# Layer 3 of a four-layer graph network: scores in rows, exponentials by head, squares exchanged through DRAM, no adding transfers

## The chip, the cores and the metric

The kernel runs on one core of a Trainium2 chip. Its time is the device time of one execution in microseconds (us); the number to compare is the median of several executions. The engines of the core are called PE (TensorE, matrix products and transpositions through them), DVE (VectorE), ACT (ScalarE), POOL (GpSimd) and SP (SyncE, which here only issues transfers). All data are 32-bit floats.

## The reference

There are 128 graphs of 128 nodes with 512 features. Four attention layers follow each other, each with a layer norm and a ReLU before it and the input added after it. Layers 0 and 2 have one head; layer 1 has two attentions, of 4 heads of 256 and of one head of 512; layer 3 has 8 heads of 64. Layer 3, which the change is about, is in short:

```python
h  = relu(layernorm(x))                                  # 128 nodes x 512
xh = (h @ W_proj).reshape(128, 8, 64)                    # values by head
a_src, a_dst = <xh, W_att[:, :64]>, <xh, W_att[:, 64:]>  # 128 x 8 each
s   = leaky_relu(a_src[i] + a_dst[j] + b, 0.2)           # by head, 128 x 128
att = softmax(where(A[i, j] > 0, s, -1e30), over j)
x   = x + relu(att @ xh)                                 # heads side by side
```

## The kernel before

Each graph is one stream of steps (`graph(b)`, line 983 and on): load, layer 0, layer 1, layer 2, layer 3, store. A graph's 128 nodes lie on the 128 partitions. Up to `FLYING = 11` graphs are in work at once. The order on every engine is made when the program is built: a scheduler (`Scheduler`, `issue`) holds a list of streams, gives each step a planned time from costs in `Step.estimate` and the buffers it needs from pools, and each time writes out the next step of the stream whose planned start is earliest, or, among those nearly as early, the one most overdue. A due time is the graph's age times the busiest engine's planned load, plus its place in the graph (`plan`, `rank`). On the chip each engine runs its instructions strictly in the written order, waiting where data are not there. A `Fork` starts a side stream, a `Join` waits for it; `Group` keeps steps together. All steps are issued at line 301, so the profile's groups are told apart by tile names.

Layers 0 and 2 call `attended`: the scores' row part is a PE transposition of a broadcast column, DVE adds the mask and takes the maximum in one instruction, ACT makes the exponentials, PE transposes them (`transposed`, with a copy by ACT) and multiplies. Layer 1 has its row part written to DRAM and read back broadcast to all partitions (`rows_in_dram`, four small writes and one load on SP), then the same by head; the 4 x 128 x 128 weights are transposed in two moves: DVE transposes all 32 x 32 squares in place, and `turned` exchanges the squares through DRAM (four writes and one load on SP).

Layer 3 before keeps the scores of each head with the source node j on the partitions, so that they go into PE without a transposition. `graph` takes the transposed mask from the PE transposition that layer 1 needs anyway, as `m3t` (11 buffers). `layer3` copies it eight times into `e` (tile of 128 x 8 x 128, 3 buffers) with one ACT instruction. PE projects (16 products of two passes), ACT copies to `fx` (tile x3), POOL adds the bias into `f`. `rows_in_dram` writes both score parts as rows; SP loads the j part into `d`, broadcast, and POOL adds the i part onto `e` with an accumulating transfer (`added`). DVE runs eight mask-and-maximum instructions on `d` for the largest score of each row and head, `mx`; POOL, ACT and POOL turn it into minus the largest score. Those go to DRAM as rows as well, and a second accumulating transfer adds them to `e` after ACT's eight Prelu instructions, which bring in the j part as a bias. One Exp over all 1024 columns follows, then PE multiplies with the values; a column of ones beside each head's values gives the sum of the weights, by which DVE divides.

The last `LATE = 5` graphs have no transfers in their chains: rows come from PE (`spread`, transpositions of broadcast columns into a bank of PSUM), and `add_rows` has DVE add them to `e`, once for the i part and once for minus the largest score.

Of the kernel before, what the change touches and what calls it, by code (L numbers as in the profile page):

```python
# [9 lines left out]
F32 = mybir.dt.float32  # L10
I32 = mybir.dt.int32
AF = mybir.ActivationFunctionType
ALU = mybir.AluOpType
# [31 lines left out]
class Step:  # L45
# [19 lines left out]
    def estimate(self, name, outs, ins, kw):  # L65

        if name == "dma_start":
            moved = size(outs[0]) * outs[0].shape[0] * 4
            if self.engine == "POOL":
                self.moves = moved / 165e3  # L70
                return 1.0, 3
            run = 4 * min(a.shape[-1] for a in outs + ins)
            self.moves = moved / (280e3 if run > 512 else 220e3)
            busy = 0.5 if max(len(a.shape) for a in outs + ins) > 2 else 0.35
            return busy, (2.2 if moved > 16384 else 0.6)
# [250 lines left out]
def kernel(  # L326
# [54 lines left out]
    def tile_of(tag, bufs, *shape):  # L381
        return Take(work, [P, *shape], tag, bufs)
# [44 lines left out]
    def setup():  # L427
# [7 lines left out]
        for c in range(KC):  # L435
            if c % 2 == 0:
                pair = yield tile_of("e3", 3, H3, P)
                pair = pair.rearrange("p h q -> p (h q)").rearrange("p (c f) -> p c f", c=2)
            w0.append(pair[:, c % 2])
            yield S.dma_start(out=w0[c], in_=l0_w[c * P : (c + 1) * P])  # L440
# [25 lines left out]
        wa = yield tile_of("e3", 3, H3, P)  # L466
        wa = wa.rearrange("p h q -> p (h q)")[:, : H3 * 2 * K3]
# [120 lines left out]
    def turned(t, squares, tag, bufs):  # L588

        yield V.transpose(squares, squares)
        f = t.shape[1] // R
        d = dram.tile([R, Q, R, f], F32, tag="turned", name="turned")
        yield Group(
            [
                S.dma_start(
                    out=d[:, :, r].rearrange("m b f -> b m f"),
                    in_=t[r * Q : (r + 1) * Q].rearrange("b (m f) -> b m f", m=R),
                )  # L600
                for r in range(R)
            ]
        )
        to = yield tile_of(tag, bufs, R * f)
        yield S.dma_start(out=to, in_=d.rearrange("m b r f -> (m b) (r f)"))
        return to
# [33 lines left out]

    def add_rows(cols, to):

        for g in range(0, cols.shape[1], 4):
            pt = yield from spread(cols[:, g : g + 4])
            part = to[:, g * P : (g + 4) * P]
            yield V.tensor_tensor(part, pt, part, ALU.add)
            give_back(pt)

    def added(to, rows):

        yield G.dma_start(out=to, in_=rows, accum_op=ALU.add)
# [120 lines left out]
    def layer1(xt, mask, late):  # L772
# [28 lines left out]
        else:  # L801
            to = yield from turned(e, e, "et1", 2)
# [57 lines left out]
    def layer3(xt, mask, mask_t, late):  # L860

# [8 lines left out]

        e = yield tile_of("e3", 3, H3, P)
        yield A.copy(e, mask_t.unsqueeze(1).to_broadcast([P, H3, P]))
        give_back(mask_t)
# [11 lines left out]
        yield G.tensor_tensor(f, fx[:, :, :E3].rearrange("p h s -> p s h"), b_l3, ALU.add)  # L885
        if late:
            fork = yield Fork(add_rows(f[:, 1], e.rearrange("p h q -> p (h q)")))
        else:
            rows = yield from rows_in_dram(repeated(f.rearrange("p s h -> p (s h)")), 2 * H3)
            d = yield tile_of("d3", 2, H3, P)  # L890
            yield S.dma_start(out=d.rearrange("p h q -> p (h q)"), in_=rows[:, : H3 * P])
            fork = yield Fork(added(e.rearrange("p h q -> p (h q)"), rows[:, H3 * P :]))

        for g in range(0, H3, 4):
            if late:
                d = yield from spread(f[:, 0, g : g + 4])
                part = d.rearrange("p (h q) -> p h q", h=4)
            else:
                part = d[:, g : g + 4]
# [3 lines left out]
                        out=part[:, j],  # L903
                        in0=part[:, j],
                        in1=mask,
# [9 lines left out]
            if late:  # L915
                give_back(d)
        give_back(mask)
        if not late:
            give_back(d)
        yield Join(fork)  # L920
# [3 lines left out]
        fork = None if late else (yield Fork(rows_in_dram(repeated(mx), H3)))  # L924
        for k in range(H3):
            yield A.activation(
                out=e[:, k, :],
                in_=e[:, k, :],
                func=AF.Prelu,
                bias=f[:, 0, k : k + 1],  # L930
                alpha=SLOPE,
            )
        ef = e.rearrange("p h q -> p (h q)")
        fork = yield Fork(add_rows(mx, ef) if late else added(ef, (yield Join(fork))))
        yield Join(fork)
        yield A.activation(out=ef, in_=ef, func=AF.Exp)
        t = yield tile_of("t", 5, D)
        for i in range(2):
# [6 lines left out]
                        lhsT=e[:, k, :],  # L945
# [16 lines left out]
        give_back(e, fx, f)  # L962
        yield V.scalar_tensor_tensor(xt, t, 0.0, xt, ALU.max, ALU.add)
# [19 lines left out]
    def graph(b):  # L983
# [9 lines left out]
        m3t = yield tile_of("m3t", FLYING, P)  # L993
# [5 lines left out]
        yield A.copy(m3t, pt[:, :P])  # L999
# [9 lines left out]
        yield from layer3(xt, m3, m3t, b >= B - LATE)  # L1009
# [65 lines left out]
```

## Time and profile before

| | |
|---|---|
| Time, median of 3 executions | 3332.38 us (3332.28 to 3333.03) |
| Profiled execution | 3333.2 us, span 3331.4 us |
| Instructions | 59808 |
| PE, DVE, ACT, POOL busy, share of the span | 99%, 83%, 74%, 36% |
| Share of 16 DMA engines: SP's queue, POOL's queue | 25.7%, 20.8% |
| Moved | 380.90 MB, mean 114 GB/s |

How to read it: the profile is one execution recorded by the hardware. PE's matmuls are pipelined and their records overlap, so that a busy PE may still be one that waits a little; the distances between starts tell more. A group is all instructions of one form on the same tiles, and its line gives engine, operation, output and inputs, shapes, count, busy time of all together, the mean of one in ns, and the idle time of the engine just before them with what ended it. PEclk is the clock that PE was granted, in tenths of full speed.

### The profile page before, as it was taken

How to read it: one execution, taken by the hardware profiler on the slowest of the kernel's cores; microseconds unless marked ns; L12 is line 12 of the kernel's file. 1: busy time of each engine (PE TensorE's matmuls, PEld its weight loads, DVE VectorE, ACT ScalarE, POOL GpSimd, SP SyncE). 2: the span in 40 equal slices, each digit the busy share in tenths (PEclk: the TensorE clock that was granted, in tenths of full speed). 3: DMA queues.
4: the chain of work that ended last, by engine and by line, in shares of the span. 5: the costliest groups of instructions: out<-in, count | busy, mean ns of one | idle time of the engine just before them, and what ended most of it. 6: DMA issues, size and time to landing. Idle time of an engine off the chain costs nothing. (4 is left out here: it accounts for less than half of the span.)

```text
span 3331.4 us, 59808 instructions
## 1 busy us (share of the span) xinstructions
PE 3286.5 (99%) x16252; PEld 2577.7 (77%) x16252; DVE 2752.8 (83%) x11063; ACT 2478.1 (74%) x6932; POOL 1208.4 (36%) x2559
## 2 busy tenths in 40 slices
PE   7999999999999999999999999999999999999997
PEld 5777777777777777777777777777777777777776
DVE  5878888888888888888888888888888888888866
ACT  4677777777777777777777777777777777777764
POOL 1233343343343343333334334334334334334321
PEclk7999999999999999999999999999999999999998
DMA  5144444454445454454545454445445545545430
GB/s 156 50 111 116 118 122 115 121 121 119 113 123 121 116 124 119 114 125 114 120 121 120 116 118 121 121 115 123 118 115 124 121 115 120 121 114 123 93 85 29
DMA packets 253730, 380.90 MB, mean 114 GB/s; under 512 B 59088, under 2 KB 138448, under 8 KB 253392
## 3 DMA queue, kind: packets, MB, share of 16 engines
q1 hardware_dynamic: 213792, 248.06, 25.7%
q0 software_dynamic: 35424, 128.99, 20.8%
q8 instruction: 130, 2.13, 0.3%
q14 instruction: 208, 1.70, 0.2%
q10 hardware_dynamic: 4176, 0.02, 0.1%
HBM read 309.35 MB, written 67.57 MB: 113 GB/s over the span
## 5 line engine op out<-in xcount | busy, mean ns | idle before, releaser
L301 PE MATMUL bank<-w2x,y 128*128 128x257 f32 x4096 | 972.1, 380 | 0.0
L301 PE MATMUL bank<-w1x,ht 128*128 128x344 f32 x3072 | 957.4, 455 | 0.7 <-ACT ht L301 0.7
L301 PEld LDWEIGHTS bank<-w2x,y 128*128 128x128 f32 x4096 | 759.4, 190 | 218.5 <-issue 119.6
L301 PEld LDWEIGHTS bank<-w1x,ht 128*128 128x128 f32 x3072 | 567.7, 191 | 243.3 <-issue 7.8
L301 ACT ACTIVATE h<-xt,st 128x512 f32<-128x512 f32 x512 | 416.5, 814 | 257.4 <-POOL st L301 256.2
L301 POOL TENSOR_SCALAR st<-st 128x1 f32<-128x1 f32 x1024 | 351.4, 347 | 661.8 <-DVE st L301 539.5
L301 ACT ACTIVATE e<-e,c 128x128 f32<-128x128 f32 x1408 | 532.7, 400 | 77.8 <-DVE e L301 59.0
L301 PE MATMUL bank<-wpx,ht 128*128 128x264 f32 x2048 | 501.9, 389 | 1.7 <-ACT ht L301 1.7
L301 PEld LDWEIGHTS bank<-wpx,ht 128*128 128x128 f32 x2048 | 390.5, 191 | 66.5 <-ACT ht L301 2.4
L301 ACT ACTIVATE e<-e,f 128x128 f32<-128x128 f32 x1152 | 386.1, 392 | 2.6 <-POOL st L301 1.5
L301 POOL DMA_DIRECT2D e<-d x246 | 233.3, 948 | 389.1 <-DMA d<-r 208.7
L301 DVE BATCH_NORM_STATS2 st<-xt 128x6 f32<-128x512 f32 x512 | 349.4, 683 | 0.0
L301 PEld LDWEIGHTS bank<-x,e 128*128 128x128 f32 x2048 | 269.4, 193 | 91.4 <-issue 56.7
L301 POOL TENSOR_TENSOR st<-st,minus_half 128x1 f32<-128x1 f32 x512 | 298.5, 585 | 29.4
L301 PE MATMUL bank<-et,xl 128*128 128x128 f32 x2048 | 270.3, 275 | 0.0
L301 PE MATMUL bank<-x,e 128*128 128x65 f32 x2048 | 259.0, 270 | 8.9 <-ACT e L301 8.9
L301 POOL TENSOR_TENSOR f<-f 128x8 f32<-128x8 f32 x128 | 30.7, 240 | 651.3 <-DVE f L301 449.1
L301 PE MATMUL bank<-h,et 128*128 128x512 f32 x512 | 263.8, 597 | 1.8 <-ACT et L301 1.8
L301 PEld LDWEIGHTS bank<-et,xl 128*128 128x128 f32 x2048 | 254.0, 192 | 4.9 <-issue 0.5
L301 DVE TENSOR_TENSOR y<-bank,b 128x512 f32<-128x512 f32 x256 | 176.1, 688 | 97.3 <-PE bank L301 95.8
L301 DVE CUSTOM_DVE_ANT_0 d<-d,m 128x128 f32<-128x128 f32 x984 | 225.3, 284 | 34.9 <-DMA d<-d 33.8
L301 POOL TENSOR_SCALAR m<-m 128x128 f32<-128x128 f32 x128 | 143.3, 1119 | 288.9 <-DVE m L301 266.1
(86 smaller groups left out, 5334.4 us busy)
## 6 DMA issues: line engine op xcount, KB each, us to landing
e<-d POOLq DMA_DIRECT2D x246, 512.0 KB, 7.1
d<-d SPq DMA_DIRECT2D x123, 512.0 KB
xt<-in_x_dram SPq DMA_DIRECT2D x128, 256.0 KB
e<-d SPq DMA_DIRECT2D x128, 256.0 KB
out_dram<-xt SPq DMA_DIRECT2D x128, 256.0 KB
turned<-e SPq DMA_DIRECT2D x492, 64.0 KB
et<-turned SPq DMA_DIRECT2D x123, 256.0 KB
at<-in_adj_dram SPq DMA_DIRECT2D x32, 256.0 KB
```

What stands on the lines that cost most here:

```text
L301: method(*args, **kw)
```

## The change

Layer 3's scores are kept with the target node i on the partitions, in rows, as layer 1's are. `m3t`, its copy, the eightfold copy into `e`, `add_rows` and `added` go away. Only the j part goes through DRAM as rows, and SP loads it straight into `e`, in an order where the 32-column pieces of all heads lie together (`heads_inside`). DVE's mask-and-maximum instructions write their sums back into `e`. ACT then runs eight Prelu with the i part as bias, and eight Exp with minus the largest score as bias, in place of one Exp. For the transposition, `turned` becomes `exchanged`, without the DVE step: layer 1 still transposes its squares before the exchange; layer 3 exchanges 128 x 1024 values first (four writes of 128 KB with runs of 1 KB, one load of 512 KB into the new tile `et3` with 2 buffers, which takes the place of `d3`), and then DVE transposes all squares from `et3` back into `e` with one instruction that also puts the pieces in order of heads. In the late graphs `spread` makes the j rows, DVE writes sums from PSUM into `e`, and PE transposes the eight heads with two copies by ACT into `ht` tiles. `layer3` takes `e` after the projection instead of before it. In the scheduler the planned delay of a small transfer goes from 0.6 to 1.3 us, which the order of everything else is made with too.

```diff
@@ -72,7 +72,7 @@
             run = 4 * min(a.shape[-1] for a in outs + ins)
             self.moves = moved / (280e3 if run > 512 else 220e3)
             busy = 0.5 if max(len(a.shape) for a in outs + ins) > 2 else 0.35
-            return busy, (2.2 if moved > 16384 else 0.6)
+            return busy, (2.2 if moved > 16384 else 1.3)
         n = max(size(a) for a in outs[:1] + ins)
         if self.engine == "PE":
             if name == "transpose":
@@ -434,8 +434,8 @@
         w0 = []
         for c in range(KC):
             if c % 2 == 0:
-                pair = yield tile_of("e3", 3, H3, P)
-                pair = pair.rearrange("p h q -> p (h q)").rearrange("p (c f) -> p c f", c=2)
+                pair = yield tile_of("e3", 3, H3 * P)
+                pair = pair.rearrange("p (c f) -> p c f", c=2)
             w0.append(pair[:, c % 2])
             yield S.dma_start(out=w0[c], in_=l0_w[c * P : (c + 1) * P])
         yield Fork(fold_u(w0))
@@ -463,8 +463,8 @@
                 out=wpx[c][:, :, E3:],
                 in_=l3_wp[c * P : (c + 1) * P].rearrange("p (h k) -> p h k", h=H3),
             )
-        wa = yield tile_of("e3", 3, H3, P)
-        wa = wa.rearrange("p h q -> p (h q)")[:, : H3 * 2 * K3]
+        wa = yield tile_of("e3", 3, H3 * P)
+        wa = wa[:, : H3 * 2 * K3]
         yield S.dma_start(out=wa, in_=l3_watt.rearrange("h k -> (h k)").partition_broadcast(P))
         yield Fork(fold_w3(wa), 6)
         for b in range(6, min(FLYING + AHEAD, B)):
@@ -585,13 +585,11 @@
         give_back(pt)
         return blocks_of(r)
 
-    def turned(t, squares, tag, bufs):
-
-
-
-        yield V.transpose(squares, squares)
+    def exchanged(t, tag, bufs):
+
+
         f = t.shape[1] // R
-        d = dram.tile([R, Q, R, f], F32, tag="turned", name="turned")
+        d = dram.tile([R, Q, R, f], F32, tag=f"exchanged{f}", name="exchanged")
         yield Group(
             [
                 S.dma_start(
@@ -637,18 +635,6 @@
             ]
         )
         return pt
-
-    def add_rows(cols, to):
-
-        for g in range(0, cols.shape[1], 4):
-            pt = yield from spread(cols[:, g : g + 4])
-            part = to[:, g * P : (g + 4) * P]
-            yield V.tensor_tensor(part, pt, part, ALU.add)
-            give_back(pt)
-
-    def added(to, rows):
-
-        yield G.dma_start(out=to, in_=rows, accum_op=ALU.add)
 
     def attention(own, rows, e, mask, exact=False):
 
@@ -799,7 +785,9 @@
         if late:
             et = yield from transposed(blocks_of(e), "et1", 2)
         else:
-            to = yield from turned(e, e, "et1", 2)
+
+            yield V.transpose(e, e)
+            to = yield from exchanged(e, "et1", 2)
             et = to.rearrange("p (r h b) -> p h r b", h=H1, b=Q)
             et = [et[:, j] for j in range(H1)]
         give_back(e)
@@ -857,8 +845,7 @@
         yield V.scalar_tensor_tensor(xt, pa, rz, xt, ALU.mult, ALU.add)
         give_back(pa, c)
 
-    def layer3(xt, mask, mask_t, late):
-
+    def layer3(xt, mask, late):
 
         h = yield from norm_relu(xt)
         ht = yield from transposed(blocks_of(h), "ht", 3)
@@ -867,10 +854,6 @@
 
         fx = yield tile_of("x3", 3, H3, E3 + K3 + 1)
         yield G.memset(fx[:, :, E3 + K3 :], 1.0)
-
-        e = yield tile_of("e3", 3, H3, P)
-        yield A.copy(e, mask_t.unsqueeze(1).to_broadcast([P, H3, P]))
-        give_back(mask_t)
         half = H3 // 2
         yield from projected(
             ht,
@@ -883,26 +866,28 @@
         f = yield tile_of("f3", 4, 4, H3)
         f, mx, rz = f[:, :2], f[:, 2], f[:, 3]
         yield G.tensor_tensor(f, fx[:, :, :E3].rearrange("p h s -> p s h"), b_l3, ALU.add)
+
+        e = yield tile_of("e3", 3, H3 * P)
         if late:
-            fork = yield Fork(add_rows(f[:, 1], e.rearrange("p h q -> p (h q)")))
+            heads = e.rearrange("p (h c b) -> p h c b", h=H3, b=Q)
         else:
-            rows = yield from rows_in_dram(repeated(f.rearrange("p s h -> p (s h)")), 2 * H3)
-            d = yield tile_of("d3", 2, H3, P)
-            yield S.dma_start(out=d.rearrange("p h q -> p (h q)"), in_=rows[:, : H3 * P])
-            fork = yield Fork(added(e.rearrange("p h q -> p (h q)"), rows[:, H3 * P :]))
+            heads = e.rearrange("p (c h b) -> p h c b", h=H3, b=Q)
+            rows = yield from rows_in_dram(repeated(f[:, 0]), H3, True)
+            yield S.dma_start(out=e, in_=rows)
+        mask3 = mask.rearrange("p (c b) -> p c b", b=Q)
 
         for g in range(0, H3, 4):
+            part = [heads[:, g + j] for j in range(4)]
             if late:
-                d = yield from spread(f[:, 0, g : g + 4])
-                part = d.rearrange("p (h q) -> p h q", h=4)
-            else:
-                part = d[:, g : g + 4]
+                pt = yield from spread(f[:, 0, g : g + 4])
+                part = pt.rearrange("p (h c b) -> p h c b", h=4, b=Q)
+                part = [part[:, j] for j in range(4)]
             yield Group(
                 [
                     V.tensor_tensor_reduce(
-                        out=part[:, j],
-                        in0=part[:, j],
-                        in1=mask,
+                        out=heads[:, g + j],
+                        in0=part[j],
+                        in1=mask3,
                         scale=1.0,
                         scalar=LOWEST,
                         op0=ALU.add,
@@ -913,27 +898,29 @@
                 ]
             )
             if late:
-                give_back(d)
+                give_back(pt)
         give_back(mask)
-        if not late:
-            give_back(d)
-        yield Join(fork)
         yield G.tensor_tensor(mx, mx, f[:, 1], ALU.add)
         yield A.activation(out=mx, in_=mx, func=AF.Prelu, alpha=SLOPE)
         yield G.tensor_scalar(mx, mx, -1.0, None, ALU.mult)
-        fork = None if late else (yield Fork(rows_in_dram(repeated(mx), H3)))
-        for k in range(H3):
-            yield A.activation(
-                out=e[:, k, :],
-                in_=e[:, k, :],
-                func=AF.Prelu,
-                bias=f[:, 0, k : k + 1],
-                alpha=SLOPE,
+        for bias, func in ((f[:, 1], dict(func=AF.Prelu, alpha=SLOPE)), (mx, dict(func=AF.Exp))):
+            for k in range(H3):
+                yield A.activation(
+                    out=heads[:, k], in_=heads[:, k], bias=bias[:, k : k + 1], **func
+                )
+        et = []
+        if late:
+            for g in range(0, H3, 4):
+                et += yield from transposed(blocks_of(e)[g : g + 4], "ht", 3)
+        else:
+            to = yield from exchanged(e, "et3", 2)
+
+            yield V.transpose(
+                e.rearrange("p (h r b) -> p r h b", h=H3, b=Q),
+                to.rearrange("p (r h b) -> p r h b", h=H3, b=Q),
             )
-        ef = e.rearrange("p h q -> p (h q)")
-        fork = yield Fork(add_rows(mx, ef) if late else added(ef, (yield Join(fork))))
-        yield Join(fork)
-        yield A.activation(out=ef, in_=ef, func=AF.Exp)
+            give_back(to)
+            et = blocks_of(e)
         t = yield tile_of("t", 5, D)
         for i in range(2):
             pa = yield bank()
@@ -942,7 +929,7 @@
                 [
                     T.matmul(
                         p3[:, k - i * half, :],
-                        lhsT=e[:, k, :],
+                        lhsT=et[k],
                         rhs=fx[:, k, E3:],
                         start=True,
                         stop=True,
@@ -960,6 +947,8 @@
             )
             give_back(pa)
         give_back(e, fx, f)
+        if late:
+            give_back(et[0], et[4])
         yield V.scalar_tensor_tensor(xt, t, 0.0, xt, ALU.max, ALU.add)
         give_back(t)
 
@@ -990,13 +979,11 @@
         yield from layer0(xt, m0)
         give_back(m0)
         m3 = yield from not_above_0(a)
-        m3t = yield tile_of("m3t", FLYING, P)
         m1 = yield tile_of("m1", 8, P)
         pt = yield bank()
         yield T.transpose(pt[:, :P], m3, ident)
         give_back(m3)
         yield V.tensor_tensor(m1, pt[:, :P], off_diag, ALU.mult)
-        yield A.copy(m3t, pt[:, :P])
         give_back(pt)
         yield from layer1(xt, m1, b >= B - LATE)
         give_back(m1)
@@ -1006,7 +993,7 @@
         yield from layer2(xt, m2)
         give_back(m2)
         m3 = yield from not_above_0(a)
-        yield from layer3(xt, m3, m3t, b >= B - LATE)
+        yield from layer3(xt, m3, b >= B - LATE)
         yield S.dma_start(out=out[b], in_=xt)
 
     adjs, xs = {}, {}
```

## The prediction

> **What bounds the kernel now.** I read the page's busy shares first, then its slices, then the same busy times in three stretches (columns: stretch, length, then busy time and count per engine, TensorE's granted clock, DMA share, GB/s), then who TensorE waited for inside those stretches.
>
> ```profile
> PE 3286.5 (99%) x16252; PEld 2577.7 (77%) x16252; DVE 2752.8 (83%) x11063; ACT 2478.1 (74%) x6932; POOL 1208.4 (36%) x2559
> ...
> PEclk7999999999999999999999999999999999999998
> ```
> ```profile
> 0.00:100.00 100.00, 77.93 (x274) 51.32 (x275) 62.88 (x211) 47.80 (x126) 14.41 (x42) 0.81 0.47 140
> 100.00:3200.00 3100.00, 3099.47 (x15388) 2436.53 (x15387) 2602.42 (x10533) 2362.70 (x6632) 1165.68 (x2442) 1.00 0.48 116
> 3200.00:3332.00 132.00, 109.08 (x593) 89.88 (x591) 87.47 (x322) 67.60 (x176) 28.32 (x75) 0.91 0.19 48
> ```
>
> PE's waits in the middle 3100 us, then in the last 132:
>
> ```profile
> PE bank L301 <- ACT et L301: 0.4, 1, 0.4
> ```
> ```profile
> PE bank L301 <- ACT e L301: 8.9, 4, 2.7
> PE bank L301 <- ACT h L301: 3.6, 4, 2.1
> PE bank L301 <- POOL f L301: 2.8, 3, 1.7
> ```
>
> A busy PE could still hide waits, since matmuls overlap, so I took start-to-start distances from PE's timeline around 1600 us: 290 ns for 344 columns, 222 for 264, 216 for 257, 430 for 512, 111 for 128 in a run, 104 for 65, 110 for one transposition. Per graph that is 24 x 0.290 + 32 x 0.216 + 16 x 0.222 + 6 x 0.43 + 16 x 0.111 + 16 x 0.104 + 15 x 0.110 = 25.1 us, and graphs do leave every 25.1 us of PE work. So the middle is PE work and nothing else: no other engine's saving can shorten it, while a new wait would lengthen it. Summing starts against these distances, PE loses 41 us in the first 100 us (weights arriving, and a half clock), 13 in the middle 3100 (0.2 in 50), 31 in the last 132. Only head, tail and PE's own instruction count can get shorter.
>
> **What the change costs on each engine.** The rows (busy total, mean ns, idle before):
>
> ```profile
> L301 ACT ACTIVATE e<-e,f 128x128 f32<-128x128 f32 x1152 | 386.1, 392 | 2.6 <-POOL st L301 1.5 <-DMA e<-d 0.8 <-DVE c L301 0.2
> L301 POOL DMA_DIRECT2D e<-d x246 | 233.3, 948 | 389.1 <-DMA d<-r 208.7 <-ACT e L301 155.6 <-issue 18.7
> L301 ACT ACTIVATE e<-e 128x1024 f32<-128x1024 f32 x128 | 134.5, 1051 | 15.3 <-DVE e L301 12.0 <-DMA e<-d 3.3
> L301 ACT COPY e<-m3t 128x1024 f32<-128x1024 f32 x128 | 132.2, 1033 | 0.0
> L301 DVE STREAM_TRANSPOSE e<-e 128x512 f32<-128x512 f32 x123 | 85.3, 693 | 2.0 <-ACT e L301 1.8
> L301 ACT COPY m3t<-bank 128x128 f32<-128x128 f32 x128 | 33.9, 265 | 38.9 <-DVE m L301 38.0
> L301 DVE STREAM_TRANSPOSE r<-f 128x32 f32<-128x32 f32 x246 | 50.8, 207 | 34.8 <-POOL f L301 26.4
> L301 DVE TENSOR_TENSOR e<-bank,e 128x512 f32<-128x512 f32 x20 | 13.3, 685 | 6.2 <-PE bank L301 5.3 <-ACT e L301 0.7
> ```
>
> *ACT*, per graph: out go two mask copies (1.03 + 0.27) and one Exp over 1024 (1.05), 2.35 us; in come eight Exps over 128 with a bias, like the e<-e,f row, 386.1/1152 = 0.335 us each, 2.68. Net +0.33: from 2362.7/3100 x 25.1 = 19.1 us of 25.1 to 19.5. [...]
>
> *DVE*: one of two 32-column transpositions goes (0.21), a 1024-column one comes. No row has it; the 32- and 512-column rows give 0.207 + 992 x (0.693 - 0.207)/480 = 1.21 us. Its operands are cut in 32-element pieces; the mask-and-max reductions are 284 ns whole (d,m) and 286 in such pieces (layer 1's e,m), so I take 1.21, with twice that, 2.4, as the upper end and the 512-column 0.69 as the lower. DVE goes from 21.1 us of 25.1 to 22.1 (23.3).
>
> *POOL* loses two adding transfers a graph, 1.9 us, and the waits in front of them, 389 us in all, which stood before the norm steps queued behind. Nobody in the middle waits for that on PE, so I credit nothing.
>
> *SP* issues 10 transfers for layer 3 instead of 9 (row writes 4, row load 1, square writes 4, square load 1); at 0.3 to 0.43 us each it stays near 8 us of 25. New on its queue is a wait for the last Exp, before the four square writes. Queued behind in the built order are the square load, the next layer-1 rows and layer 1's own square writes; who waits is PE, for layer 1's matmuls. These come 60.6 us of PE work after the projection that feeds them, 47.8 before. DMA bytes stay near 381 MB, without the 20.8% share of the adding queue.
>
> *Layer 3's chain.* From its projection to its attention matmuls the built orders put 36.5 us of PE work before and 62.8 after. The need: x copy, bias, r, row writes and load as the chain of waits has them near 3213 us (0.37 + 0.43 + 0.21 + 1.34 + 1.44 + 4.80) 8.6; eight reductions 2.3; POOL, ACT, POOL 1.0; sixteen activations 5.4; four square writes 1.7 to issue and 1.4 (as a row write) to 4.8 (as a load) to land; load 4.8; transposition 1.2 to 2.4. That is 26 to 32 us, against 62.8: over 30 us of cover for queueing. Before it was some 24 (the adding transfers land in 7.1) against 36.5, and PE never waited. So I cost the middle at 0 in the likely case. If the cover goes, 0.1 us a graph costs 12 us over some 117 graphs.
>
> *PE*: each of the five late graphs loses 24 spread transpositions and gains 8 + 8, 40 fewer at 0.107 = -4.3 us. The built orders put 1.3 of that after the last graph's layer-1 projection, where PE waits anyway; the other 3.0 lie where PE is nearly full. **-3.0.**
>
> **The tail.** The last graph alone sets the end; the late chain runs on chip. Timeline lines of before:
>
> ```profile
> 3297.72 2.66 DVE L301 TENSOR_TENSOR e<-bank,e 128x512 f32<-128x512 f32 x4
> ...
> 3300.43 0.69 DVE L301 BATCH_NORM_STATS2 st<-xt 128x6 f32<-128x512 f32 x1
> ...
> 3323.06 3.68 PE L301 MATMUL bank<-x,e 128*128 128x65 f32 x16 [2.74 <-ACT e L301]
> ...
> 3327.45 0.69 DVE L301 SCALAR_TENSOR_TENSOR xt<-t,xt 128x512 f32<-128x512 f32 x1
> ```
>
> Four adds stand between the last graph's layer-2 result and its statistics; they go, and a 0.2 us mask step stays: -2.4. Then the projection no longer meets PE at half clock behind its neighbour's matmuls, and its f is out about 3307.7 instead of 3311.1: together -3.4. From there: spreads 0.5, eight reductions 3.0, mx 0.9, sixteen activations with two copies of its neighbour in between 5.9, transposition, copy, second transposition, copy 2.2, last matmuls 1.0: last step near 3322, against 3327.45: -5.5. Against it, ACT carries +0.33 + 1.05 us more per late graph (Exps, and two copies of transposed squares at 0.58, without the fills), all in program order before h and ht; over the last two graphs I charge +1, between 0 (hidden in ACT's idle half) and +5 (all of it on the path), near the low end since the walk above already has ACT's queue in it. In the trace the last 16 matmuls ran at 230 ns, not 104, after a 2.7 us wait. [...]
>
> **The head** is reordered (no mask copies, a small write planned at 1.3 us, not 0.6). Nothing prices it: of its 41 us some 13 are waits that an order can move, so -4 to +4, taken 0.
>
> **Sum.** The profiled execution took 3333.2 us (span 3331.4 and 1.8 around it), 0.8 over the median 3332.38. 3333.2 - 3.0 - 5.5 + 1 + 0 = 3325.7; against the median that is 0.8 more than it should be, so I say 3325.5, 0.21% under it. From no change a measurement here can tell about 0.2%, 6.7 us.
>
> **Rivals.**
> *A wait each period (slower).* The new order repeats exactly every graph, so a step that is late is late 117 times. The tightest place: layer 2's scores are transposed, copied by ACT and needed by PE 0.86 us later, ACT having an Exp, a Relu and a Prelu (1.4 us) in front. Before had the same 0.9 us at its tightest and lost nothing; but ACT and DVE are now fuller, and DVE would stand in front of a late square load. It decides from 0.06 us a graph; at 0.2 the time is 3325.5 + 23 = 3349. For: DVE at 88 to 93%. Against: over 30 us of cover, DVE waits of a microsecond for PE left in the period. Chance 0.24.
> *The tail is ACT's.* All +5 on the path and no gain behind the adds: 3333.2 - 3.0 + 5 = 3335. Chance 0.08.
> *No visible effect*: late PE saving and tail swallowed by other waits of the last 132 us, 3332. Chance 0.10.
> *The forecast*, tail and late graphs shorten and the middle holds: chance 0.58, own range 3317 to 3331 (tail and head each ± 4).
>
> **How the numbers follow.** 0.2% under the median is 3325.7, which cuts the forecast's own case a little above its middle; the waits of the head leave more room below than above, so I put six tenths of it under the line: faster 0.58 x 0.6 = 0.35, rounded up to 0.36. Slower: 0.23 of the first rival, 0.03 of the second, 0.26. The rest, 0.38, is within 0.2%. Eight in ten: from 3316 (forecast with its best head and tail) to 3348, which cuts the first rival near 0.18 us a graph.
>
> **What would show it.** Right: PE's waits in 100 to 3200 still under 1 us in all, its instructions 16212, DVE near 88%, POOL near 29%, no software queue, and the last stretch with fewer than 31 us lost. Wrong: PE waits for ACT et or ht some hundred times, or DVE waiting on e3's square load; a first 100 us with more than 45 us lost; the new transposition over 2.4 us.

## The result, and the profile after

The changed kernel takes **3321.62 us** (median of 13 executions, 3319.59 to 3327.11) against 3331.06 us (13 executions, 3328.96 to 3333.03) of the kernel before on the same chip: ratio **0.9975**, 95% interval 0.9967 to 0.9984. By the medians it is faster by 9.4 us. The profiled execution of it took 3326.81 us (span 3325.0), 5.2 over its own median, so the pair of profiles shows only 6.4 us of the difference; why is the first thing that the experiments had to settle.

Busy shares of the changed kernel, the clock that PE was granted, and SP's queue:

```profile
PE 3291.0 (99%) x16212; PEld 2577.6 (78%) x16212; DVE 2783.9 (84%) x11043; ACT 2552.8 (77%) x7582; POOL 863.9 (26%) x2313
...
PEclk7999999999999999999999999999999999999998
...
q1 hardware_dynamic: 286608, 376.04, 38.4%
```

PE's instructions are the 16212 expected. POOL falls from 36% to 26%, the software queue is gone, and SP's queue carries what both carried. The three stretches (length, then busy time and count of PE, weight loads, DVE, ACT, POOL, then the granted clock, DMA share, GB/s):

```profile
0.00:100.00 100.00, 81.05 (x270) 52.97 (x271) 63.55 (x211) 45.33 (x119) 15.00 (x39) 0.76 0.47 141
100.00:3200.00 3100.00, 3099.84 (x15368) 2435.12 (x15367) 2646.33 (x10525) 2427.25 (x7218) 826.31 (x2204) 1.00 0.40 116
3200.00:3332.00 132.00, 110.08 (x578) 89.54 (x576) 74.06 (x308) 80.26 (x246) 22.62 (x70) 0.91 0.17 53
```

The middle is full, as before; the list of PE's waits there is empty. DVE is at 85.4% of it, ACT at 78.3%. The new and enlarged groups of layer 3 (busy together, mean ns, idle before):

```profile
L301 ACT ACTIVATE e<-e,f 128x128 f32<-128x128 f32 x2176 | 740.7, 393 | 0.0
...
L301 DVE STREAM_TRANSPOSE e<-et 128x1024 f32<-128x1024 f32 x123 | 153.1, 1245 | 4.1 <-issue 0.8 <-DMA et<-exchanged 0.4
```

The transposition of 1024 columns takes 1.245 us and has waited 0.4 us in all for its square load. The activations e<-e,f, which the eight Exps more per graph join, have 0.340 us of busy time each (740.7/2176), where it was 0.335 before; neighbours among them start 292 ns apart in both kernels (the median), and the rest is the tail of the last record before other work comes between.

A product of the kernel stands in the trace as two records, a transposition as one: the projection's eight products are the 16 that the description of the kernel before names. What is called a product here is a record. To see where the time went, I take the sum of start-to-start distances of PE's instructions in each profile, less what each would take in a run of its like (0.842 ns per column, as the 290 ns for 344 columns, and at least 105 ns, as the 65-column products): what is over is time lost by PE, what is taken off is its work. "Last 130" runs from 130 to 60 us before the end.

| Profile (us) | span | PE work | lost in first 100 | lost in the middle | lost in last 130 | lost in last 60 |
|---|---|---|---|---|---|---|
| before | 3331.4 | 3236.2 | 40.9 | 14.0 | 10.5 | 20.4 |
| after | 3325.0 | 3231.8 | 41.3 | 18.9 | 2.5 | 21.1 |
| difference | -6.4 | -4.3 | +0.4 | +4.9 | -8.0 | +0.7 |

The other 9.4 us of each span lie before PE's first start and after its last. Two of these differences were not in the prediction: the middle loses more though nobody waits, and the end gains not in the last graph's chain but earlier.

**The end.** PE's timeline of before (start, duration, instruction, count; in brackets the idle time before it and what ended it):

```profile
3229.74 0.66 PE L301 MATMUL bank<-ident,h 128*128 128x128 f32 x4 [0.47 <-ACT h L301]
3231.69 3.40 PE L301 MATMUL bank<-wpx,ht 128*128 128x264 f32 x8 [1.30 <-ACT ht L301]
3234.89 4.00 PE L301 MATMUL bank<-w2x,y 128*128 128x257 f32 x16
...
3252.71 1.11 PE L301 MATMUL bank<-ident,h 128*128 128x128 f32 x4 [2.09 <-ACT h L301]
...
3254.50 3.89 PE L301 MATMUL bank<-wpx,ht 128*128 128x264 f32 x8
```

and of after, in the same part of the run:

```profile
3242.30 1.90 PE L301 MATMUL bank<-w2x,y 128*128 128x257 f32 x8
...
3251.95 0.66 PE L301 MATMUL bank<-ident,h 128*128 128x128 f32 x4 [0.75 <-ACT h L301]
3253.29 2.05 PE L301 MATMUL bank<-wpx,ht 128*128 128x264 f32 x8 [0.68 <-ACT ht L301]
```

Before, PE twice stood before a layer-3 norm (h, then its transposed ht), and each wait drew a second cost: the eight products of 264 columns took 3.40 us instead of 1.95, the sixteen of 257 columns 4.00 instead of 3.63; behind the second wait the eight took 3.89. PE was granted 0.50 of its clock from 3232.3 to 3235.6 us and from 3252.8 to 3259.5. After, the waits are shorter and the eight take 2.05, at a granted 1.00 from 3252 to 3256.

**The last graph.** DVE's steps of after, statistics to last step, with the projection between:

```profile
3295.38 0.69 DVE L301 BATCH_NORM_STATS2 st<-xt 128x6 f32<-128x512 f32 x1
...
3300.72 5.39 PE L301 MATMUL bank<-wpx,ht 128*128 128x264 f32 x16
...
3316.70 3.67 PE L301 MATMUL bank<-x,ht 128*128 128x65 f32 x16
...
3321.16 0.69 DVE L301 SCALAR_TENSOR_TENSOR xt<-t,xt 128x512 f32<-128x512 f32 x1
```

From statistics to last step it is 25.8 us, against 27.0 before (3300.43 to 3327.45). The sixteen projections took 5.39 us; before they took 4.53.

**The middle.** PE's timeline around 1600 us, after:

```profile
1601.51 1.00 PE L301 MATMUL bank<-x,e 128*128 128x65 f32 x8
1602.35 1.11 PE L301 MATMUL bank<-et,xl 128*128 128x128 f32 x8
1603.30 0.60 PE L301 MATMUL bank<-ident,h 128*128 128x128 f32 x4
...
1619.91 1.05 PE L301 MATMUL bank<-et,xl 128*128 128x128 f32 x8
1620.80 1.90 PE L301 MATMUL bank<-w2x,y 128*128 128x257 f32 x8
```

and before:

```profile
1610.14 1.00 PE L301 MATMUL bank<-x,e 128*128 128x65 f32 x8
1610.98 0.28 PE L301 MATMUL bank<-ident,m 128*128 128x128 f32 x1
1611.09 0.27 PE L301 MATMUL bank<-ident,e 128*128 128x128 f32 x1
...
1623.87 1.06 PE L301 MATMUL bank<-et,xl 128*128 128x128 f32 x8
1624.76 1.02 PE L301 MATMUL bank<-h,et 128*128 128x512 f32 x2
```

Eight layer-1 products take 0.89 us from start to next start (1619.91 to 1620.80, and 1623.87 to 1624.76), but 0.95 (1602.35 to 1603.30) where they follow the 65-column products of layer 3. The first of the eight is 164 ns from the next, not 109 to 112. In the new order that happens 117 times: 117 x 0.056 = 6.6 us. Before, both 65-column runs of a graph were followed by a transposition, which lost 8 ns. What the weight loads show of this is in the last section.

### The profile page after: what moved, and what is told of

Read it like the earlier page. It is cut to its first block, busy times and chain, and to the rows that moved or that the text cites. A ratio compares the mean times of both kernels' runs of the same rounds, so it can differ in the third digit from the quotient of the medians.

```text
span 3325.0 us, 59473 instructions
## 1 busy us (share of the span) xinstructions
PE 3291.0 (99%) x16212; PEld 2577.6 (78%) x16212; DVE 2783.9 (84%) x11043; ACT 2552.8 (77%) x7582; POOL 863.9 (26%) x2313
## 4 chain that ended last, share of the span: by engine, by line
PE 98%; DVE 1%; ACT 1%; POOL 0%; issue 0%; DMA 0%; ACTq 0%; POOLq 0%; DVEq 0%
PE bank L301 98%; POOL st L301 0%; DVE st L301 0%; DVE e L301 0%; ACT ht L301 0%; ACT h L301 0%; DVE products L301 0%; DVE xt L301 0%; DVE t L301 0%; DMA a<-in_L_gnn_a_dram 0%; ACT e L301 0%; DVE m L301 0%; DVE wpx L301 0%; DVE c L301 0%; ACT et L301 0%
## 5 line engine op out<-in xcount | busy, mean ns | idle before, releaser
L301 ACT ACTIVATE e<-e,f 128x128 f32<-128x128 f32 x2176 | 740.7, 393 | 0.0
L301 POOL TENSOR_SCALAR st<-st 128x1 f32<-128x1 f32 x1024 | 306.2, 306 | 838.2 <-DVE st L301 765.5
L301 PEld LDWEIGHTS bank<-wpx,ht 128*128 128x128 f32 x2048 | 372.0, 191 | 88.5 <-issue 33.5
L301 POOL TENSOR_TENSOR st<-st,minus_half 128x1 f32<-128x1 f32 x512 | 337.4, 667 | 11.8
L301 DVE CUSTOM_DVE_ANT_0 e<-e,m 128x128 f32<-128x128 f32 x1496 | 334.6, 284 | 0.0
L301 ACT COPY ht<-bank 128x512 f32<-128x512 f32 x274 | 158.3, 578 | 215.3 <-PE bank L301 214.9
L301 PEld LDWEIGHTS bank<-x,e 128*128 128x128 f32 x1968 | 248.4, 192 | 6.3
L301 DVE SCALAR_TENSOR_TENSOR t<-t,bank 128x512 f32<-128x512 f32 x128 | 88.0, 687 | 193.8 <-ACT bank L301 193.8
L301 PE MATMUL bank<-x,e 128*128 128x65 f32 x1968 | 246.8, 268 | 0.0
L301 ACT ACTIVATE t<-t 128x512 f32<-128x512 f32 x256 | 161.5, 631 | 95.8 <-DVE t L301 95.5
```

Of the source, the lines that this page charges most:

```text
L301: method(*args, **kw)
```

## The experiments

Ratios are to runs of the kernel before on the same chip. The table gives, for the profile of each, where PE lost its time; the first three columns are the timed runs.

| Run | median us | ratio | 95% interval | first 100 | middle | last 130 | last 60 |
|---|---|---|---|---|---|---|---|
| late_only | 3323.75 | 0.9979 | 0.9969 to 0.9988 | 40.7 | 14.7 | 8.1 | 17.4 |
| steady_only | 3326.38 | 0.9986 | 0.9977 to 0.9995 | 37.1 | 19.4 | 1.2 | 21.7 |
| before_13 | 3334.34 | 1.0011 | 1.0002 to 1.0020 | 39.0 | 21.7 | 3.3 | 23.0 |
| after_06 | 3321.26 | 0.9973 | 0.9964 to 0.9983 | 37.0 | 21.5 | 2.5 | 19.7 |
| after_again | 3322.31 | 0.9972 | 0.9961 to 0.9984 | 35.7 | 18.8 | 2.5 | 20.2 |
| after_3t | 3418.78 | 1.0260 | 1.0245 to 1.0276 | 42.2 | 114.6 | 3.3 | 18.6 |
| after_late_adds | 3324.11 | 0.9984 | 0.9974 to 0.9993 | 35.4 | 18.9 | 2.8 | 24.1 |
| after_late_pe | 3318.19 | 0.9965 | 0.9952 to 0.9978 | 38.8 | 18.9 | 1.7 | 15.7 |
| before_late3 | 3333.00 | 1.0006 | 0.9997 to 1.0016 | 42.4 | 13.6 | 13.6 | 25.2 |
| after_late3 | 3322.18 | 0.9974 | 0.9963 to 0.9984 | 35.1 | 19.0 | 2.0 | 26.0 |
| before_late8 | 3334.64 | 1.0009 | 1.0000 to 1.0019 | 40.5 | 14.5 | 1.4 | 21.3 |
| after_late8 | 3328.70 | 0.9995 | 0.9986 to 1.0005 | 39.5 | 19.3 | 5.8 | 17.6 |

### One part alone: the late graphs, the steady ones, the planned delay

late_only keeps the old layer 3 for 123 graphs and gives the last five the new one; steady_only the reverse (its test is `b >= B - LATE`):

```diff
-        yield from layer3(xt, m3, m3t, b >= B - LATE)
+        if b < B - LATE:
+            yield from layer3_old(xt, m3, m3t, b >= B - LATE)
+        else:
+            yield from layer3(xt, m3, b >= B - LATE)
```

> The kernel before with layer 3 of the last five graphs alone as changed (order up to the last 6% as before). Theory T (the gain is PE's 40 fewer transpositions and a shorter tail): the whole gain, ratio 0.9970 to 0.9985; in the profile about 4 us less PE work and 5 to 8 us less lost after 3200 us, the middle at 14 us lost as before. Theory M (the gain comes from the middle or the head, where adding transfers and their waits on POOL went): ratio 0.999 to 1.0005.

> The changed kernel with the last five graphs in layer 3 as before (m3t is made for those alone). Theory T: no gain, ratio 0.999 to 1.003: the middle loses about 19 us at PE where before lost 14, the last stretch about 31. Theory M: the whole gain, 0.9965 to 0.9985.

before_13 changes the planned delay alone, after_06 takes that one line back:

```diff
-            return busy, (2.2 if moved > 16384 else 0.6)
+            return busy, (2.2 if moved > 16384 else 1.3)
```

> The kernel before with the planned delay of small transfers at 1.3 us in place of 0.6, nothing else. Theory T: within 0.15% (0.9985 to 1.0015), differences only in head and tail order. Theory D (the new planned delay makes the better order and so the gain): 0.9970 to 0.9985.

> The changed kernel with the planned delay back at 0.6 us. Theory T: the gain stays, 0.9965 to 0.9990. Theory D: the gain is gone, 0.9990 to 1.002, PE waiting for late rows in the middle.

Measured: the late graphs alone give 7.5 us (3331.21 to 3323.75), the steady ones alone 4.8 (3331.21 to 3326.38), together 9.4. The intervals are some 3 us wide to each side, so the times alone don't prove that the two share something; the columns show where they would. late_only, with the planned delay of before, has 4.3 us less PE work and loses 3.0 less in the last 60 us, the stretch in which the prediction put the gain, and 2.4 less in the last 130; its head is as before. steady_only, with the new planned delay, loses 9.3 less in the last 130, and 3.8 less in the head, and pays 5.4 in the middle; its PE work is that of before. So the changed steady graphs shorten the end too: the last of them is still at work, beside the late ones, 66 us before the end (its new transposition starts at 3259.3 in after), and with the new steps and the new order PE's waits for h and ht there go. Which of the two does it this run doesn't tell. Another order is enough: before_13, which has the new planned delay and none of the new steps, loses 3.3 in the last 130 us instead of 10.5, but pays for it with 7.7 us more in the middle and 2.6 more in the last 60. And the new delay isn't needed: after_06, with the new steps and the old delay, loses 2.5. The planned delay by itself gains nothing: on the kernel before it loses some 3 us (3334.34 against 3331.21), on the changed kernel it makes no difference (3321.26 against 3321.62). With the same planned delay on both sides the changed kernel is faster by 12.7 us at 1.3 (3334.34 to 3321.62) and by 10.0 at 0.6 (3331.21 to 3321.26; the first pair is from two sets of runs, whose runs of before have medians of 3331.21 and 3331.06). What the delay moves is the middle: with 1.3 on before, the first product behind the 65-column ones comes with 53.2 ns of loss 119 times, and with 0.6 on after with 55.4 ns 118 times, each a different product (h,et and w2x,y in place of et,xl).

### The same kernel once more

> The changed kernel once more, unaltered, for a second profile. Theory H (its runs spread over 7 us because the first 100 us differ from execution to execution): this profile loses 37 or 41 us in the first 100 us, the middle (19 us lost) and the last stretch (23 to 24) as in the first profile to 1 us. Rival (the middle or the end differs): the first 100 us lose 41 again and the difference lies elsewhere. Ratio 0.9965 to 0.9985 in both.

Measured: 3322.31 us, ratio as the first time. Its profiled execution took 3320.22 us, 6.6 less than the first profile of the same program. Middle and end repeat within 0.1 and 0.9 us; the first 100 us lose 35.7 instead of 41.3. The windows of the first profile (length, PE, weight loads, DVE, ACT, POOL, granted clock, DMA share, GB/s):

```profile
45.00:60.00 15.00, 14.33 (x49) 8.86 (x48) 11.65 (x36) 4.96 (x11) 3.12 (x7) 0.91 0.00 0
60.00:80.00 20.00, 14.78 (x40) 8.54 (x39) 15.05 (x64) 11.07 (x34) 4.60 (x9) 0.79 0.12 40
80.00:100.00 20.00, 15.79 (x55) 10.54 (x54) 18.02 (x46) 14.11 (x44) 1.29 (x3) 0.70 0.21 59
```

and of the second:

```profile
45.00:60.00 15.00, 13.86 (x51) 8.54 (x49) 13.98 (x42) 6.44 (x12) 5.44 (x11) 1.00 0.10 28
60.00:80.00 20.00, 12.33 (x37) 7.20 (x38) 18.32 (x81) 14.68 (x51) 2.53 (x7) 0.87 0.15 46
80.00:100.00 20.00, 18.19 (x77) 13.38 (x77) 17.62 (x38) 11.53 (x29) 3.14 (x8) 0.88 0.27 66
```

The granted clock from 60 to 100 us was 0.79 and 0.70 in one, 0.87 and 0.88 in the other, and PE got through 297 instructions in 100 us instead of 270. PE's waits in these 100 us add up to 18.9 us in the first profile and 19.9 in the second, so it is not waiting that differs, and the granted clock is 0.76 there on the mean against 0.85. So a first profile may stand several us from its median by the head alone. PE's written order of the first 280 instructions is one and the same in seven profiles with the change and delay 1.3 (after, after_again, steady_only, after_late_adds, after_late_pe, after_late3, after_late8), and one and the same in four with the old one. They lose 41.3, 35.7, 37.1, 35.4, 38.8, 35.1 and 39.5, mean 37.6, against 40.9, 40.7, 42.4 and 40.5, mean 41.1. So the head is worth some 3.5 us on the mean, though not in the pair of profiles first compared. With it the sum is -4.3 (work) - 3.5 (head) + 4.9 (middle) - 7.3 (end) = -10.2, against -9.4 by the medians.

### How much room DVE has

The new transposition three times, the same values each time:

```diff
-            yield V.transpose(
...
+            for _ in range(3):
+                yield V.transpose(
...
```

> The changed kernel with the new transposition by VectorE done three times in a row in each of the 123 graphs (the same values written again), 2.5 us more for DVE in each 25.1 us. Theory T (the middle is PE's alone): ratio to before within 0.2% of the changed kernel's 0.9975, DVE near 95% busy in the middle, PE still without waits. Rival (DVE is next in line): at 95% DVE makes PE wait, 0.1 to 1 us a graph, ratio 1.000 to 1.03.

Measured: 88 us more than before, 96 more than after_again. The waits of PE in 100 to 3200 us, the transposition's group, and that stretch:

```profile
PE bank L301 <- ACT ht L301: 67.7, 114, 1.0
```
```profile
L301 DVE STREAM_TRANSPOSE e<-et 128x1024 f32<-128x1024 f32 x369 | 459.0, 1244 | 7.5 <-issue 0.4
```
```profile
100.00:3200.00 3100.00, 3031.06 (x14891) 2374.10 (x14890) 2807.57 (x10445) 2346.68 (x7010) 908.74 (x2142) 1.00 0.39 113
```

That 2.5 us more DVE work a graph would stay hidden was wrong: PE now waits once in every graph, 114 times, 0.6 us each, and DVE is no more than 90.6% busy. The wait that the first rival looked for is thus there, one or two transpositions further on, and it is for ht, a copy by ACT behind DVE's steps: on the chain that ended last around 1600 us DVE's steps follow each other from 1617.35 to 1624.77 with no gap over 0.03 us, and after a short step and the copy by ACT the matmuls start at 1625.94. The changed kernel sits between this and the old one: 1.0 us a graph was free; 3.5 us (three times 1.245 less the 0.2 that went) cost 0.8 us a graph (96 us over 123 graphs). Where between the two the cover ends was not tried.

### Two steps of the end given back

after_late_adds puts into each late graph of the changed kernel four DVE additions of 512 columns (into an unread tile), as the old layer 3 had them (in this run, the next one and late_only the scheduler also gives steps beyond the length of the first graph's list the last due time in it, since late graphs there are longer):

```diff
             if late:
                 pt = yield from spread(f[:, 0, g : g + 4])
+                yield V.tensor_tensor(products, pt, products, ALU.add)
+                yield V.tensor_tensor(products, pt, products, ALU.add)
```

> The changed kernel with four DVE additions of 512 columns put back into layer 3 of each of the last five graphs (into a scratch tile, 2.7 us of DVE each, as many as went). If the adds in front of the last graph's statistics were what the tail lost, as the prediction said (-2.4, and -3.4 up to its scores): 2 to 4 us slower than the changed kernel, the last 60 us losing 2 to 4 us more. If the tail's gain is a matter of the order in which the scheduler writes the last 120 us: within 1.5 us or either way.

after_late_pe gives back the PE work, 8 unread transpositions per late graph:

```diff
+        for g in range(0, H3 if late else 0, 4):
+            pt = yield from spread(f[:, 1, g : g + 4])
+            give_back(pt)
```

> The changed kernel with eight spread transpositions, which nobody reads, put back into layer 3 of each of the last five graphs: 40 in all, 4.3 us of PE work, as many as went. By the prediction 3.0 of these are on the path: 2.5 to 4.5 us slower than the changed kernel. If they fall into PE's waits of the last 130 us: 0 to 1.5 us slower.

Measured: with the adds 3324.11 us, 1.8 more than after_again, and the last 60 us lose 24.1 instead of 20.2. That is not far from what the prediction gave the four (2.4), but the difference of the medians is within their spread (ratio 1.0005, 0.9999 to 1.0020, from the two sets of runs). With the 40 transpositions given back the kernel is not slower: 3318.19, the lowest of all, though from five executions between 3317.28 and 3325.64; the last 60 us lose 15.7 instead of 20.2, perhaps because the added work stands where PE waited. That those 4.3 us lie on the path, as the prediction had 3.0 of them, this run speaks against; it can't exclude it, since the added steps also rewrite the order of the end. Its interval and that of the changed kernel overlap (0.9952 to 0.9978, and 0.9967 to 0.9984), so it isn't proved to be the faster one.

### Other ends of the run: is it the change, or luck of the order?

After all this a rival had to be met: that the end's gain has nothing to do with the change's steps, and comes from another written order only. `LATE` rewrites the end for both kernels, here with 3 and likewise with 8:

```diff
-LATE = 5
+LATE = 3
```

> The kernel before with LATE = 3 in place of 5: only the last three graphs have chains without transfers, so the written order of the last 200 us is another one. It is the partner of the next run; the pair asks whether the change is worth something whatever the order at the end is. Theory S (the change's own steps shorten the end: four DVE adds before the last graph's statistics, shorter late chains): the partner after/before keeps a ratio near 0.9975, within 0.9960 to 0.9990, though this run by itself may land anywhere from 3320 to 3350. Theory O (which waits meet in the last 130 us is an accident of the written order): this run and its partner differ from the pair with 5 by as much as the change is worth, and the ratio of the pair lies outside 0.9960 to 0.9990, above 1.0 included. By both, the stretch from 100 to 3200 us loses 14 to 15 us against start-to-start distances, as before.

> The changed kernel with LATE = 3. Theory S: 6 to 12 us less than the run with LATE = 3 of the kernel before. Theory O: anywhere from 10 us less to 10 us more. By both, the middle loses 18 to 20 us (4 to 5 more than in its partner, the first product of layer 1's attention behind 65-column products), and with it a median near 3322 if the end is alike to that with 5 late graphs.

> The kernel before with LATE = 8. Eight late graphs carry 3 x 24 more spread transpositions in layer 3 alone (0.107 us each, 7.7 us of PE work, and more in layer 1), so PE work alone lets one expect 3340 to 3355. Partner of the next run, the same question as for the pair with 3.

> The changed kernel with LATE = 8. In late graphs it has 8 fewer transpositions each than the kernel before: 64 x 0.107 = 6.8 us less PE work instead of 4.3. Theory S: the ratio to the kernel before with 8 is 0.996 to 0.9985 (0.9975, or 0.9967 if the late PE work counts). Theory O: outside that, on either side.

Measured, changed over old with the same LATE: with 3, 3322.18/3333.00 = 0.9968 (0.9958 to 0.9978, from resampling the runs of both), with 8, 3328.70/3334.64 = 0.9982 (0.9979 to 0.9991). With 5 it is 0.9972 by the same measure. In three orders of the end the change wins, by 10.8 (3), 9.4 (5) and 5.9 us (8): both ratios fall in the band that theory S had named, so theory O falls as to the sign. As to the mechanism it is half right. PE's waits from 3200 to 3280 us in before_late3,

```profile
PE bank L301 <- ACT h L301: 4.9, 3, 2.1
PE bank L301 <- DVE f L301: 1.9, 1, 1.9
PE bank L301 <- ACT ht L301: 0.9, 2, 0.7
```

and in before_late8,

```profile
PE bank L301 <- ACT e L301: 0.3, 1, 0.3
PE bank L301 <- DVE f L301: 0.2, 1, 0.2
```

show that the old kernel has the stall before its end with 3 and 5 late graphs, and not with 8 (13.6, 10.5 and 1.4 us lost in the last 130). Where it is there, the change takes it away (2.0, 2.5), as the new planned delay alone nearly does (3.3 in before_13); where it isn't, there is none to take (5.8), and the gain is smaller. With 8 what the profiles show is 6.9 us less PE work (3245.2 to 3238.3, 64 transpositions), 1.0 in the head and 3.7 in the last 60 us, against 4.7 in the middle and 4.4 in the last 130: 2.5 in all where the medians differ by 5.9; the profiled execution of after_late8 was 2.9 over its median. That before_late8 would take 3340 or more by its PE work was a miss: it has 9.0 us more (3245.2 against 3236.2), and most of that is regained by the missing stall.

## Why the prediction was right, and where it wasn't

*The outcome.* The prediction said 3325.5 us and 0.21% under; it is 3321.62 and 0.28% under the runs beside it. No wait arose in the middle, no rival came to pass, and the sum came from head, late graphs and end. The terms, however, were made up differently, and that the sum came within 4 us is in part luck: the two largest of the measured differences, +4.9 in the middle and -8.0 ahead of the last 60 us, are in none of its terms, and they pull opposite ways.

- *The middle at 0.* No wait arose: the list of PE's waits is empty, the new wait on SP's queue for the last Exp reached nobody, and DVE waited 0.4 us in all for the square load. The cover was there. What failed is the sentence under it, that a stretch of "PE work and nothing else" can only be lengthened by a wait. The order lengthened it by 4.9 us: 117 products behind 65-column products cost 56 ns more. The PE rows were priced one by one, each in a run of its own kind, and the order after the change was there to be read, but not read for neighbours. Its 104 ns for 65 columns is a mean that hides them: the first of eight is 56 to 59 ns from the second, the others 112 from the next.
- *PE work, -4.3, of which 3.0 counted.* The work fell by 4.3 in the table. That it shortens the run wasn't shown: given back, it cost nothing visible.
- *The tail, -5.5, through the last graph's chain.* From statistics to the last step it became 1.2 us shorter, not 3.1 (5.5 less the 2.4 ahead of the statistics). The part from f on was right: 3306.60 to 3321.16, 14.6 us, against 14.3 walked out and 16.6 before. The part that failed is "the projection no longer meets PE at half clock behind its neighbour's matmuls": it met it again, 5.39 us for 16 against 16 x 0.222 = 3.55. That is 1.84 us, all that was missing. PE had just waited 2.27 us for h, and was granted 0.69 of its clock from 3299 to 3303. The removed adds were priced 2.4; giving four back cost 1.8, uncertain.
- *What was not seen*: the stall of PE for late graphs' norms at 3229 and 3252 us in before, 8 us of the gain. The tail had been read from the last graph backwards; the list of waits for the last 132 us named h with 3.6 us, and where those stood was not looked up. What followed them at half clock is in no list of waits.
- *ACT, +1.* The row that gave 0.335 was misread: busy time over count has the tail of each block's last record in it, and neighbours start 292 ns apart (the median), before and after. In the middle ACT's busy time rose by 64.6 us (2362.70 to 2427.25), 0.52 a graph, not 0.33. What the Exps cost on the path at the end can't be told from the order's own effect.
- *The head, 0, within 4 either way.* Some -3.5 on the mean, inside the bound, but +0.4 in the first pair of profiles.
- *DVE near 88%.* It is 85.4%. The transposition cost 1.245 against 1.21, as worked out from two rows, and the dropped one saved its 0.2; yet DVE's busy time in the middle rose by 43.9 us (2602.42 to 2646.33), 0.36 us a graph, not 1.0. Several other DVE groups are recorded shorter (reductions of layer 3 and layer 1 together 336.7 us before, 327.3 after). POOL is at 26%, not 29%: besides the transfers, its mask step of 128 x 128 is recorded at 549 ns on the mean, against 1119 before (128 of them, 73 us). Busy time counts overlapping records once. The durations of all DVE records in the middle, added up, rise by 106 us (3206 to 3312), 0.86 a graph, so most of the miss is overlap, which an order changes by itself: before_13, with the steps of before, has DVE busy for 2537.68 us there. Why the records of unchanged steps got shorter on two engines together is open.
- *The first rival*, a wait in every period, was right in kind and is close: with 2.5 us more on DVE it costs 96 us. Its sign in the profile, PE waiting for ht some hundred times, appeared there word for word.

## What to carry to other kernels

Where one engine is full, price its instructions by what stands next to them in the new order, not only by their own row: here a run of eight 65-column products cost the product behind it 53 to 56 ns, and a transposition 7 to 9. Read a tail in the list of waits with their places, and add what ran at half clock behind each wait (eight products took 3.40 us in place of 1.95 here), before the chain of the last item is walked. Before a small difference is explained from one pair of profiles, profile the same program again: here the head alone moved it by 5.6 us, more than half of what the change is worth.

## What was not expected of the hardware

**Short products and their neighbours.** Eight products of 65 columns take 0.84 us to the next instruction's start, 104 to 105 ns each on the mean, but not evenly: the first is 56 to 59 ns from the second, the other seven follow at 112, as products of 128 columns do. The product after the last of them is longer by 53.2 ns (512 columns, 119 times in before_13), 55.4 (257 columns, 118 times in after_06) or 56.4 (128 columns, 117 times in after); a transposition in that place is longer by 7 to 9 ns (237 times in before). So the cost depends on what follows, not on the 65-column products alone. The records of the weight loads show how. From one short product to the next, and on to a product behind them, the loads start 112 ns apart, from the third on 55 ns after the start of the product ahead of it, which is what 65 columns take at 0.842 ns each; in a run of 128 columns a load starts with the product ahead of it (2 to 3 ns after). So the run and what follows go at the pace of the loads, 112 ns, and what the first short product saves the product behind the run pays back. The load of a transposition starts 2 ns after the last short product and 58 ns after that product's load, so that the saving is kept. Why it may start earlier no run here shows. An order with a transposition behind both runs of every graph would by these numbers save some 6 us in the changed kernel, an estimate (117 times about 50 ns); it wasn't tried.

**Half clock behind some waits.** PE ran at half speed behind a wait of 1.30 us that came 0.65 us behind another of 0.47 (granted 0.50 from 3232.3 to 3235.6 in before, 3.40 us for eight products of 264 columns in place of 1.95), behind one of 2.80 us (granted 0.50 from 3285 to 3288 in after), and for part of the time behind one of 2.27 (0.69 from 3299 to 3303 in after). Not every such wait did it at once: in before the eight products of 65 columns behind waits of 2.25 and 2.19 us (at 3287.62 and 3301.52) took 1.11 and 1.10 us at a granted 1.00, against 1.00 us in the middle and 1.80 at a granted 0.50 (at 3304.20). In 3310 to 3316 us of after PE was busy 4.03 of 6 us, and from 3316 to 3321 it was granted 0.50. What decides between these cases no run here shows.

**DVE at 90.6% already stalls PE.** In after_3t, with its work in a fixed written order, DVE was late without being full: one step of a period came too late by 0.6 us (67.7 us over 114 waits), and the period grew by more than that (96 us over 123 graphs, 0.8 us each).
